# Attention's neighbour lists built earlier: sorted in the second product, eight of fifteen tiles' lists in the convolution

## The chip, the cores and the metric

The kernel runs on one core of one Trainium2 chip. A time is the device time of one execution in microseconds (us); three runs of the kernel before gave 1941.38, 1943.07 and 1949.31 us, and the median, 1943.07 us, is the figure to compare with. The profile is one further execution, recorded by the hardware profiler. It names the engines PE (matrix products; PEld its weight loads), DVE (vector), ACT (scalar), POOL (GpSimd) and SP (which here only issues DMAs). Each engine carries out its own instructions in the order in which the program gives them.

## The reference, cut to what matters

Four graph layers follow one another on x of shape 8 x 2048 x 64, with a random 0/1 adjacency of 2048 nodes whose entries are dense in its first rows and columns and sparse elsewhere. Each layer normalises x, applies ReLU, and adds its result to x.

- Layer 0: hyperedge attention, and a product of the adjacency with the features.
- Layer 1: a Chebyshev graph convolution. With A the adjacency, it forms A h and A (A h), and applies to h, A h and 2 A (A h) - h a weight that is a sum over 16 embedding values of each node.
- Layer 2: three steps, each a product of the adjacency with the state, then a small two-layer network.
- Layer 3: attention of each node over its neighbours:

```
adj = adj.at[jnp.diag_indices(N)].set(1.0)
e = leaky_relu(e_src[:, :, None] + e_dst[:, None, :]); e = adj[None] * e
h_prime = einsum('bij,bjd->bid', softmax(e, axis=-1), h)
```

Layer 3 needs, for every node, a list of its neighbours. The lists depend on the adjacency alone, so they can be built at any time before layer 3.

## The kernel before, in words

Nodes are held in 16 tiles of 128 (`NT`, `P`), a chunk is 512 nodes (`CW`), and the eight batches with 64 features make a row of 512 floats. The adjacency is not multiplied densely: nodes 0 to 383 are three dense "hub" tiles, and the rest are blocks that a list names (`LISTED`, 13 blocks for tile 0, then 7, 6, 5 and 4 or 3). Class `Feed` runs such a product. For each listed block it gathers 128 rows by an indirect DMA from POOL (line 2615), ACT rounds them to a high part (`part_hi`, 2632), DVE subtracts to get the low part (`part_lo`, 2633), and PE multiplies both into `acc`. DVE then adds the node's own row (`z`, 2676).

The stages that matter, with their place in the profiled execution:

- **Second product** (`layer1_near`, about 607 to 713 us): A h, tile by tile, through `Feed`. The convolution's first part for one column pair (`early`) follows it.
- **Convolution** (`convolution_near`, about 740 to 1225 us): over four chunks ("places") in the order 1, 0, 2, 3; in each, over four batch pairs q; in each, over eight blocks b taken by twos. Each (b, half) takes a PSUM bank `pk` (six buffers), two PE products, one DVE instruction for `y` (bias and embedding, line 1835; three buffers), and an addition of `y` into `half` (line 1842). The additions are on POOL, except those of the last block (`own = b == NBLK - 1`), which are on DVE. While one place is convolved, `product(place + 1)` advances the third product, A (A h), for the next chunk, by `advance()` twice per two blocks. Finished pairs are folded into x by PE (`fold_up`) some blocks later through the list `waiting`. The last place has no product ahead and sends layer 2's first messages instead.
- **Layer 2** (`layer2_near`, about 1225 to 1665 us): three steps of 16 tiles, each through `Feed`, with messages for the next step sent to DRAM after each tile (`u`, line 1874). The third step also projects and scores the chunks for layer 3.
- **Layer 3** (`layer3_near`, from about 1665 us).

The lists are made by a generator, `neighbours` (line 1994 on), all of it within the first two steps of layer 2. First it sorts the nodes by degree (`ranks`, line 483, then `by_rank`, line 527), and stores the order in DRAM (`order3`). Then, for tiles 1 to 15 of the sorted nodes, POOL gathers the 128 rows of links (2018), DVE multiplies them with the column numbers (2022), and takes the largest eight by MAX8 (2028), removing them with MATCH_REPLACE (2031) where more than eight are needed. `NEAR` gives the neighbours per tile, so tiles 1 to 8 need 3, 2, 2, 2, 2, 1, 1, 1 rounds of MAX8, and tiles 9 to 15 one each. `near_step()` calls the generator once per group of listed blocks, 22 times a step; what is left is drained ahead of the third step.

The order of the work is what the program's text gives, with a planner that moves an instruction where its buffers and operands are ready earlier or later in the planner's own reckoning; generators are how the text interleaves one stage with another.

Of the kernel before, what the change touches and what calls it, by code (L numbers as in the profile page):

```python
# [7 lines left out]
F = mybir.dt.float32  # L8
BF = mybir.dt.bfloat16

F12 = mybir.dt.float32r
I32 = mybir.dt.int32
# [7 lines left out]
P = 128  # L20
NB = 8
N = 2048
D = 64
NP = NB // 2
NT = N // P
R = P // NP
CW = 512
# [5 lines left out]
NBLK = DE * D // P  # L33

HELD = [16, 15, 10, 6, 3, 1, 1, 1, 1, 1, 1, 1]


NEAR = [None, 20, 14, 12, 10, 9, 8, 8, 7, 6, 6, 5, 5, 4, 4, 3]
TIED = [1 + sum(n > j for n in NEAR[1:]) for j in range(NEAR[1] + 1)]
FIRST = [sum(NEAR[1:t]) for t in range(NT + 1)]  # L40
# [6 lines left out]
F16 = mybir.dt.float16  # L47
# [88 lines left out]
class Kernel:  # L136
# [1527 lines left out]
    def layer1_near(self, slots, k2, far):  # L1664

        nc, tc, a = self.nc, self.tc, self.a
        self.steps = Steps(self, k2)
        lists = self.lists
        xe, xo = self.chebyshev(slots)
        ah = Halves(slots, "ah", ("q4", "q5"), True)  # L1670
        lo, hi = slice(0, D), slice(D, P)
        ident = self.ident
        lists.open(far.enter_context(
            tc.tile_pool(reuse_waits="tile", name="dense", bufs=1, side="right")
        ))
        with (
            tc.tile_pool(reuse_waits="tile", name="k1", bufs=1) as k,
            tc.tile_pool(reuse_waits="tile", name="conv_ps", bufs=1, space=PSUM) as ps,
        ):
            conv = Conv(self, slots, k, ps)  # L1680
            with tc.tile_pool(reuse_waits="tile", name="cheb", bufs=2) as w:
                hub = Hub(w, "first_hub")
                for t in range(HUBS):
                    hub.fill(self, t, ah(t))

                def turn(t):
                    s = slice(t * P, (t + 1) * P)
                    pz = ps.tile([P, NP, P], F, name="pz", tag="pk", bufs=6)
                    for q in range(NP):
                        nc.tensor.transpose(pz[:, q], ah(t)[:, q * P : (q + 1) * P], ident)  # L1690
                    for i in range(2):
                        qs = slice(2 * i, 2 * i + 2)
                        nc.scalar.copy(xo.tiles[i][lo, :, s], pz[lo, qs])
                        nc.vector.tensor_copy(xe.tiles[i][hi, :, s], pz[hi, qs])

                feed = Feed(self, lists, w, self.sent[0], lambda jt: ah(jt))
                for t in range(NT):
                    acc = ps.tile([P, CW], F, name="acc", bufs=2)
                    feed.target(acc, t, hub)
                    if t < HUBS:  # L1700
                        nc.scalar.copy(ah(t), acc)
                        lists.hub.fill(self, t, ah(t))
                    else:
                        feed.finish(ah(t), ah(t), acc, t)
                    nc.sync.dma_start(self.sent[1][t * P : (t + 1) * P], ah(t))
                    if t > 0:
                        turn(t - 1)
                    if t == NT // 2:
                        conv.begin()
                turn(NT - 1)  # L1710
                for _ in range(8):
                    next(conv.early)
            self.convolution_near(slots, k, ps, conv)

    def convolution_near(self, slots, k, ps, conv):
# [7 lines left out]
        with tc.tile_pool(reuse_waits="tile", name="conv", bufs=2) as w:  # L1723
# [60 lines left out]
            for _ in conv.early:  # L1784
                pass
            steps.prepare(bank)
            for place, ch in enumerate(chunks):
# [16 lines left out]
                for q in range(NP):  # L1804
# [6 lines left out]
                    for blk in range(0, NBLK, 2):  # L1811
# [15 lines left out]
                        for b in (blk, blk + 1):  # L1827
                            for half in range(2):
                                acc = accs[half]
                                new = begun or b > 0  # L1830
                                y = w.tile([P, CW], F, name="y", bufs=3) if new else acc
                                if begun:
                                    nc.vector.tensor_mul(y, pks[b, half], emb[:, b])
                                else:
                                    nc.vector.scalar_tensor_tensor(  # L1835
                                        y, pks[b, half], bias[:, b : b + 1], emb[:, b],
                                        op0=OP.add, op1=OP.mult,
                                    )
                                if new:
                                    own = b == NBLK - 1  # L1840
                                    add = nc.vector if own else nc.gpsimd
                                    add.tensor_add(acc, acc, y)  # L1842
# [39 lines left out]
    def layer2_near(self, slots, k2):  # L1882
# [3 lines left out]
        with (  # L1886
# [5 lines left out]
            own_w, seen, bias = self.steps.own, self.steps.seen, self.steps.bias  # L1892
            other = Hub(k, "other_hub")
            hubs = [lists.hub, other, lists.hub]
            near = self.neighbours(k, lambda: ps.tile([P, CW], F, name="p2"), slots)
            last = Scores(self, slots, k, w, ps)
            accs, late = {}, []

# [92 lines left out]
                    pass  # L1991
            last.end()

    def neighbours(self, k, bank, slots):

        nc = self.nc
        order = k.tile([P, 2, NT], I32, name="order")
        w = Parts(slots.tile([P, 2 * N], F, name="sort", tag="q4"))  # L2000
        rank = self.ranks(w, bank, 1, NEAR[1])
        yield
        self.by_rank(w, bank, rank, order)
        nc.sync.dma_start(self.order3, order)
        yield
        near = self.near
        words = slots.tile([P, 2, N], F, name="near_rows", tag="q4")
        rows = words[:, 0].bitcast(BF).rearrange("p (i n) -> p i n", i=2)
        named = words[:, 1].bitcast(F16).rearrange("p (i n) -> p i n", i=2)
        words = slots.tile([P, 2, N], F, name="line", tag="q5")  # L2010
        whole = words[:, 0].bitcast(I32)
        line = words[:, 1, : N // 2].bitcast(F16)
# [3 lines left out]
        for t in range(1, NT):  # L2016
            raw, row = rows[:, t % 2], named[:, t % 2]
            nc.gpsimd.indirect_dma_start(
                raw, None, self.links[:],
                bass.IndirectOffsetOnAxis(ap=order[:, 1, t : t + 1], axis=0),  # L2020
            )
            nc.vector.tensor_mul(row, raw, line)
            yield
            most = -(-NEAR[t] // 8)
            top = k.tile([P, 24], F, name="top", bufs=2)
            for i in range(most):
                eight = top[:, 8 * i : 8 * i + 8]
                nc.vector.max(out=eight, in_=row)
                yield
                if i + 1 < most:  # L2030
                    nc.vector.match_replace(
                        out=row, in_to_replace=eight, in_values=row, imm_value=0.0
                    )
# [647 lines left out]
class Conv:  # L2681
# [5 lines left out]
    def __init__(self, kern, slots, k, ps):  # L2687
# [19 lines left out]
        for j in range(2):  # L2707
# [9 lines left out]
        self.accs = [  # L2717
            [k.tile([P, CW], F, name=f"early{q}_{half}") for half in range(2)]
            for q in range(self.EARLY)
        ]  # L2720
        self.early = self.first_part()

    def bank(self):
# [18 lines left out]
    def first_part(self):  # L2742

        nc = self.nc
        s = slice(self.CHUNKS[0] * CW, (self.CHUNKS[0] + 1) * CW)
        for q in range(self.EARLY):
            for b in range(NBLK):
                for half, src in enumerate(self.xs):
                    pk = self.bank()
                    self.kern.mm(pk, self.w01[half][:, b * P : (b + 1) * P], src(q)[:, s])  # L2750
                    acc = self.accs[q][half]
                    y = self.k.tile([P, CW], F, name="early_y", bufs=2) if b else acc
# [502 lines left out]
```

## Time and profile before

| What | us |
|---|---|
| Median of three runs | 1943.07 |
| The profiled execution's own time | 1993.83 |
| Its span, first to last instruction | 1992.1 |
| PE busy over the span | 1714.6 (86%) |
| DVE busy | 1407.7 (71%) |
| POOL busy | 1047.7 (53%) |
| ACT busy | 819.8 (41%) |
| MAX8, 21 instructions | 48.0 |
| MATCH_REPLACE, 6 instructions | 13.7 |
| The lists' multiplications, 15 instructions | 18.3 |
| Last blocks' additions on DVE, 30 instructions | 33.4 |
| Additions of `y` on POOL, 180 instructions into `half` | 230.9 |

Shares of busy time are averages over stages with different limits, so the stages are read one by one: for a stretch of time, the view of windows gives the busy microseconds of every engine with the number of instructions, the PE clock granted, and the share of time that the DMA engines were busy. A group of instructions is shown as its line, engine and operation, what it writes and reads, its count, the busy microseconds and the mean in ns of one, and then the idle time of its engine just ahead of it with what ended that idle time. The view of waits lists who waited for whom. The chain of work that ended last is followed back from the last instruction; in this execution it reaches back to about 1260 us. The profiler slows the program: the profiled execution is 2.6% longer than the median.

### The profile page before, as it was taken

The page shows a single profiled execution, that of the slowest core. Times are in us where ns is not written, and L with a number is a line of the kernel's source. Part 1 is how long each engine was busy: PE and PEld are TensorE (multiplying, and loading weights), DVE is VectorE, ACT ScalarE, POOL GpSimd, SP SyncE. Part 2 cuts the span into 40 slices and gives each one's busy share as a digit, 9 for nine tenths or more (in the row PEclk, how much of TensorE's full clock was granted, in tenths as well). Part 3 has the DMA queues.
Part 4 walks back from the last instruction along what each step waited for, and adds up shares of the span by engine and source line. Part 5 has one row for each costly group of instructions (what it writes and reads, how often), then busy time and mean ns, then how long its engine had stood idle before and what let it go on. Part 6 is the DMA issues. An engine that isn't in the chain of part 4 may idle for free. (4 is left out here: it accounts for less than half of the span.)

```text
span 1992.1 us, 22431 instructions
## 1 busy us (share of the span) xinstructions
PE 1714.6 (86%) x7094; PEld 979.9 (49%) x7098; DVE 1407.7 (71%) x2307; ACT 819.8 (41%) x1650; POOL 1047.7 (53%) x1007
## 2 busy tenths in 40 slices
PE   6888999898888788999999998788787899398884
PEld 2446766663234544444444443466576665244432
DVE  6888788764667787677766566889776675276774
ACT  5722445445566643212120101555555663185300
POOL 1101466668645645776755554563663440767760
PEclk8888999998897997999999998899799898698997
DMA  9641223336436753242220211687677674746555
GB/s 342 262 117 45 75 93 113 103 110 217 127 134 188 238 178 106 64 122 69 74 85 27 88 50 54 218 255 240 201 246 246 190 236 147 249 122 187 169 152 189
DMA packets 127226, 305.22 MB, mean 153 GB/s; under 512 B 29536, under 2 KB 33392, under 8 KB 121968
## 3 DMA queue, kind: packets, MB, share of 16 engines
q0 software_dynamic: 45328, 149.60, 24.8%
q1 hardware_dynamic: 79456, 149.81, 22.2%
q10 hardware_dynamic: 2304, 4.20, 0.6%
q8 instruction: 60, 0.98, 0.2%
q14 instruction: 78, 0.64, 0.1%
HBM read 240.40 MB, written 63.14 MB: 152 GB/s over the span
## 5 line engine op out<-in xcount | busy, mean ns | idle before, releaser
L2615 POOL DMA_INDIRECT raw<-sent,index x300 | 321.3, 1071 | 302.0 <-DVE part_lo L2633 124.6
L2632 ACT CAST part_hi<-raw 128x512 fp32r<-128x512 f32 x352 | 213.0, 619 | 336.0 <-PE acc L177 226.9
L2633 DVE TENSOR_TENSOR part_lo<-raw,part_hi 128x512 fp32r<-128x512 f32 x352 | 264.3, 775 | 113.5 <-ACT part_hi L2632 60.7
L177 PE MATMUL pk<-q,w 128*128 128x512 f32 (+1 forms) x768 | 307.6, 619 | 2.0 <-DVE q L1731 0.9
L1842 POOL TENSOR_TENSOR half<-half,y 128x512 f32<-128x512 f32 x180 | 230.9, 1312 | 117.2 <-DVE y L1835 116.5
L177 PE MATMUL acc<-q,ident 128*128 128x512 f32 x416 | 209.4, 629 | 42.1 <-issue 17.3
L177 PE MATMUL acc<-part_lo,weights 128*128 128x512 f32 x365 | 169.0, 465 | 38.0 <-DVE part_lo L2633 32.2
L177 PE MATMUL acc<-part_hi,weights 128*128 128x512 f32 x365 | 174.4, 481 | 28.4 <-issue 14.1
L177 PEld LDWEIGHTS pk<-q,w 128*128 128x128 f32 (+1 forms) x768 | 117.5, 193 | 156.3 <-issue 121.5
L1835 DVE SCALAR_TENSOR_TENSOR y<-pk,bias,q 128x512 f32<-128x512 f32 x210 | 148.0, 743 | 55.5 <-PE pk L177 37.5
L2944 POOL DMA_INDIRECT ring<-f_rows,near x121 | 138.0, 1141 | 70.2 <-issue 29.9
L177 PEld LDWEIGHTS acc<-q,ident 128*128 128x128 f32 x416 | 78.9, 200 | 121.5 <-issue 70.9
L177 PEld LDWEIGHTS acc<-part_lo,weights 128*128 128x128 f32 x365 | 74.1, 203 | 91.7 <-DVE part_lo L2633 61.4
L2324 POOL TENSOR_TENSOR q<-q,beta 128x512 f32<-128x512 f32 x57 | 76.1, 1337 | 71.3 <-DVE beta L2300 32.9
L177 PEld LDWEIGHTS acc<-part_hi,weights 128*128 128x128 f32 x365 | 73.2, 200 | 79.9 <-issue 49.6
L3015 DVE TENSOR_TENSOR q<-ring,e 128x1024 f32<-128x1024 f32 x58 | 70.1, 1218 | 30.2 <-remote 13.3
L177 PE MATMUL pp<-adj,x_ind_hi 128*128 128x512 f32 x256 | 90.5, 470 | 0.5 <-DVE q L872 0.3
L2601 ACT CAST hub_weights<-dense 128x384 fp32r<-128x384 uint8 x80 | 40.5, 511 | 88.5 <-PE acc L177 84.6
L292 DVE RECIPROCAL std<-std 128x512 f32<-128x512 f32 (+1 forms) x17 | 53.7, 3161 | 30.9 <-ACT std L291 30.9
L2324 POOL TENSOR_TENSOR q<-q,coef 128x512 f32<-128x512 f32 x57 | 63.1, 1108 | 21.2 <-DVE q L2347 16.9
L2532 POOL DMA_INDIRECT listed_raw<-in_adjT_dram,cell x60 | 63.4, 1057 | 16.5 <-issue 16.2
L177 PE MATMUL pp<-adj,x_ind_lo 128*128 128x512 f32 x256 | 72.0, 400 | 0.0
(504 smaller groups left out, 3485.9 us busy)
## 6 DMA issues: line engine op xcount, KB each, us to landing
rows<-in_adj_dram SPq DMA_DIRECT2D x16, 1024.0 KB
adj_t<-in_adjT_dram SPq DMA_DIRECT2D x64, 256.0 KB
own<-sent SPq DMA_DIRECT2D x52, 256.0 KB
raw<-sent SPq DMA_DIRECT2D x52, 256.0 KB
sent<-u SPq DMA_DIRECT2D x48, 256.0 KB
q<-x SPq DMA_DIRECT2D x9, 1024.0 KB
links<-squares POOLq DMA_DIRECT2D x16, 512.0 KB
sent<-q SPq DMA_DIRECT2D x32, 256.0 KB
```

Of the source, the lines that this page charges most:

```text
L177: self.nc.tensor.matmul(out, lhsT, rhs, start=start, stop=stop)
L292: nc.vector.reciprocal(std, std)
L1835: nc.vector.scalar_tensor_tensor(y, pks[b, half], bias[:, b : b + 1], emb[:, b], op0=OP.add, op1=OP.mult,)
L1842: add.tensor_add(acc, acc, y)
L2324: self.nc.gpsimd.tensor_tensor(x, x, by.unsqueeze(2).to_broadcast([P, NB, D]), op=OP.mult)
L2532: self.kern.behind(nc.gpsimd.indirect_dma_start(raw[:, i], None, rows, bass.IndirectOffsetOnAxis(ap=self.cell[:, c + i : c + i + 1], axis= ...
L2601: self.nc.scalar.copy(to, self.lists.dense[:, :, i * P : (i + 1) * P])
L2615: self.nc.gpsimd.indirect_dma_start(raw, None, self.rows[:], bass.IndirectOffsetOnAxis(ap=self.lists.index[:, c : c + 1], axis=0),)
L2632: nc.scalar.copy(hi, raw)
L2633: nc.vector.tensor_sub(lo, raw, hi.bitcast(F))
L2944: self.nc.gpsimd.indirect_dma_start(to, None, self.kern.f_rows[:], bass.IndirectOffsetOnAxis(ap=index, axis=0))
L3015: nc.vector.tensor_tensor(y.rearrange("n i (b f) -> n i b f", b=NB), block[:, i : i + 2, : NB * D].rearrange("n i (b f) -> n i b f", b=NB) ...
```

## The change

The sort moves into a new function, `order_nodes`, which is advanced at tiles 2, 3 and 4 of the second product. `neighbours` now takes the order, a range of tiles and its buffers, gathers one tile ahead, and multiplies in place. Tiles 1 to 8 (`NEAR_EARLY = 9`) are listed in the convolution from its second place on, once per two blocks; tiles 9 to 15 in layer 2, which reads the order back from DRAM. The last blocks' additions, on DVE until now, join the others on POOL. The two buffers of the convolution's early part become one tile that the lists' rows use afterwards.

```diff
+NEAR_EARLY = 9
...
+                sorting = self.order_nodes(conv.bank, conv.order)
                 feed = Feed(self, lists, w, self.sent[0], lambda jt: ah(jt))
                 for t in range(NT):
...
                         turn(t - 1)
+                    if t > 1:
+                        next(sorting, None)
...
+                if place == 1:
+                    words = k.tile([P, 4 * CW], F, name="near_rows", tag="early", bufs=1)
+                    near = self.neighbours(
+                        steps.k, conv.order, range(1, NEAR_EARLY),
+                        words.bitcast(BF).rearrange("p (i n) -> p i n", i=2),
+                        words.bitcast(I32), w.tile([P, N], F16, name="line", bufs=1),
+                    )
...
                                 if new:
-                                    own = b == NBLK - 1
-                                    add = nc.vector if own else nc.gpsimd
-                                    add.tensor_add(acc, acc, y)
+                                    nc.gpsimd.tensor_add(acc, acc, y)
+                        next(near, None)
                         if q == NP - 1 and not ends:
...
+            for _ in near:
+                pass
             while waiting:
...
-            near = self.neighbours(k, lambda: ps.tile([P, CW], F, name="p2"), slots)
+            order = k.tile([P, 2, NT], I32, name="order")
+            nc.sync.dma_start(order, self.order3)
+            words = slots.tile([P, 2, N], F, name="near_rows", tag="q4")
+            near = self.neighbours(
+                k, order, range(NEAR_EARLY, NT),
+                words[:, 0].bitcast(BF).rearrange("p (i n) -> p i n", i=2),
+                words[:, 0].bitcast(I32), words[:, 1, : N // 2].bitcast(F16),
+            )
...
+    def order_nodes(self, bank, order):
+        rank = order[:, 1].bitcast(F)
+        with self.tc.tile_pool(reuse_waits="tile", name="sort", bufs=1) as w:
+            self.nc.vector.tensor_copy(rank, self.ranks(w, bank, 1, NEAR[1]))
         yield
+        with self.tc.tile_pool(reuse_waits="tile", name="sorted", bufs=1) as w:
+            self.by_rank(w, bank, rank, order)
         yield
+        self.nc.sync.dma_start(self.order3, order)
+        yield
+
+    def neighbours(self, k, order, tiles, rows, whole, line):
+        nc, near = self.nc, self.near
         nc.gpsimd.iota(whole, pattern=[[1, N]], base=1, channel_multiplier=0)
         nc.vector.tensor_copy(line, whole)
         yield
+        def fetch(i):
+            if i < len(tiles):
+                t = tiles[i]
+                nc.gpsimd.indirect_dma_start(
+                    rows[:, i % 2], None, self.links[:],
+                    bass.IndirectOffsetOnAxis(ap=order[:, 1, t : t + 1], axis=0),
+                )
+
+        fetch(0)
+        for i, t in enumerate(tiles):
+            fetch(i + 1)
+            row = rows[:, i % 2].bitcast(F16)
+            nc.vector.tensor_mul(row, rows[:, i % 2], line)
             yield
...
+        early = k.tile([P, 4, CW], F, name="early", tag="early", bufs=1)
+        self.accs, self.ys, self.turn = [[early[:, 0], early[:, 1]]], early[:, 2:], 0
+        self.order = k.tile([P, 2, NT], I32, name="order")
```

More of the change, by code (lines that the diff above doesn't have):

```diff
@@ L1786, in convolution_near @@
             steps.prepare(bank)
+            near = iter(())
             for place, ch in enumerate(chunks):
@@ L1992, in layer2_near @@
             last.end()
[L1994 to L2001, printed above, removed]
+    def order_nodes(self, bank, order):
+        rank = order[:, 1].bitcast(F)
+        with self.tc.tile_pool(reuse_waits="tile", name="sort", bufs=1) as w:
+            self.nc.vector.tensor_copy(rank, self.ranks(w, bank, 1, NEAR[1]))
         yield
-        self.by_rank(w, bank, rank, order)
-        nc.sync.dma_start(self.order3, order)
+        with self.tc.tile_pool(reuse_waits="tile", name="sorted", bufs=1) as w:
+            self.by_rank(w, bank, rank, order)
         yield
[L2006 to L2012, printed above, removed]
+        self.nc.sync.dma_start(self.order3, order)
+        yield
+    def neighbours(self, k, order, tiles, rows, whole, line):
+        nc, near = self.nc, self.near
         nc.gpsimd.iota(whole, pattern=[[1, N]], base=1, channel_multiplier=0)
@@ L2015, in neighbours @@
         yield
[L2016 to L2022, printed above, removed]
+        def fetch(i):
[10 more added lines that the diff above has]
+            nc.vector.tensor_mul(row, rows[:, i % 2], line)
             yield
@@ L2025, in neighbours @@
             top = k.tile([P, 24], F, name="top", bufs=2)
-            for i in range(most):
-                eight = top[:, 8 * i : 8 * i + 8]
+            for j in range(most):
+                eight = top[:, 8 * j : 8 * j + 8]
                 nc.vector.max(out=eight, in_=row)
                 yield
-                if i + 1 < most:
+                if j + 1 < most:
                     nc.vector.match_replace(
@@ L2716, in __init__ @@
         self.xs = kern.chebyshev(slots)
[L2717 to L2720, printed above, removed]
+        early = k.tile([P, 4, CW], F, name="early", tag="early", bufs=1)
+        self.accs, self.ys, self.turn = [[early[:, 0], early[:, 1]]], early[:, 2:], 0
+        self.order = k.tile([P, 2, NT], I32, name="order")
         self.early = self.first_part()
@@ L2751, in first_part @@
                     acc = self.accs[q][half]
-                    y = self.k.tile([P, CW], F, name="early_y", bufs=2) if b else acc
+                    y = self.ys[:, self.turn % 2] if b else acc
+                    self.turn += b > 0
                     nc.vector.scalar_tensor_tensor(
```

## The prediction

> **What bounds the kernel now.** I first cut the span into stages by the lines at work, and read the view of windows: the second product, the convolution's second and third places, and layer 2's steps 0, 1 and 2.
>
> ```profile
> core 0: us, PE busy (x) PEld busy (x) DVE busy (x) ACT busy (x) POOL busy (x), PEclk, DMA share, GB/s
> 607.00:713.00 106.00, 87.21 (x328) 55.62 (x326) 78.10 (x128) 72.62 (x155) 65.56 (x60) 0.91 0.76 231
> ...
> 891.00:1003.00 112.00, 111.07 (x353) 46.95 (x353) 78.18 (x97) 18.80 (x37) 72.52 (x60) 1.00 0.26 79
> 1003.00:1112.00 109.00, 107.97 (x346) 44.02 (x344) 76.00 (x99) 13.68 (x28) 66.08 (x53) 1.00 0.19 57
> ...
> 1245.00:1385.00 140.00, 114.58 (x615) 89.61 (x616) 119.85 (x169) 80.81 (x160) 74.54 (x67) 0.93 0.74 236
> 1385.00:1525.00 140.00, 113.50 (x580) 89.31 (x579) 110.38 (x147) 80.45 (x160) 76.44 (x71) 0.90 0.74 238
> 1525.00:1665.00 140.00, 126.35 (x592) 87.51 (x591) 88.24 (x161) 78.53 (x160) 57.69 (x58) 0.94 0.63 201
> ```
>
> The convolution is PE's: 99% busy, DVE about 70%. In steps 0 and 1 nobody is full: DVE 120 and 110 of 140, PE 114. Step 2 does more PE work (126) in the same 140 with DVE at 88. So steps 0 and 1 are long for their PE work, and I asked what PE waits for there, by the waits of 1252 to 1390, then of 1385 to 1525 (total us, times, longest).
>
> ```profile
> PE acc L177 <- DVE part_lo L2633: 9.6, 10, 2.8
> PE pz L1920 <- DVE z L2676: 4.8, 5, 2.2
> ```
>
> ```profile
> PE acc L177 <- DVE part_lo L2633: 13.5, 8, 2.7
> PE pz L1920 <- DVE z L2676: 1.5, 2, 0.8
> ```
>
> With 1.7 that step 0's groups put to MAX8 itself, PE idles 16.1 us for DVE in step 0 and 15.0 in step 1; step 2's group of the same products shows 0.2. The longest waits, 2.7 and 2.8 us, are about one list instruction long. These are DVE's groups in 1245 to 1385 and in 1385 to 1525:
>
> ```profile
> L2028 DVE MAX8 top<-q 128x8 f32<-128x2048 f16 x10 | 22.8, 2285 | 0.0
> L2031 DVE MATCH_REPLACE8 q<-top,q 128x2048 f16<-128x2048 f16 x6 | 13.7, 2276 | 0.0
> ...
> L2022 DVE TENSOR_TENSOR q<-q,q 128x2048 f16<-128x2048 bf16 x5 | 6.1, 1219 | 0.9 <-issue 0.9
> ```
>
> ```profile
> L2028 DVE MAX8 top<-q 128x8 f32<-128x2048 f16 x11 | 25.2, 2287 | 0.0
> L2022 DVE TENSOR_TENSOR q<-q,q 128x2048 f16<-128x2048 bf16 x10 | 12.2, 1216 | 0.0
> ```
>
> Last, DVE's groups in the convolution, 800 to 1225:
>
> ```profile
> L1835 DVE SCALAR_TENSOR_TENSOR y<-pk,bias,q 128x512 f32<-128x512 f32 x206 | 145.3, 743 | 55.5 <-PE pk L177 37.5 <-POOL half L1842 16.1 <-PE side L177 0.5
> L2633 DVE TENSOR_TENSOR part_lo<-raw,part_hi 128x512 fp32r<-128x512 f32 x42 | 51.3, 1228 | 30.1 <-ACT part_hi L2632 30.1
> L1842 DVE TENSOR_TENSOR half<-half,y 128x512 f32<-128x512 f32 x30 | 33.4, 1119 | 7.8 <-POOL half L1842 5.9
> ```
>
> DVE's idle time before `y` is mostly for PE: slack to put lists into. A `part_lo` takes 1.23 us here and 0.69 in layer 2.
>
> **What the Trainium skill says.** "SBUF — State Buffer", Who interferes with whom: a DVE instruction with two SBUF inputs contends with a GpSimd one that reads SBUF, and one with at most one SBUF input outside the two-port modes does not. The trace agrees: `part_lo` and DVE's additions (1.12 us) are stretched beside POOL's additions, and `y` from PSUM (0.743) is not. MAX8 and MATCH_REPLACE read one tensor, so I leave them at 2.28 us in the convolution; no run yet shows that. The lists' multiplication reads two and may pay as `part_lo` does. "TensorE: Matmul & The Clock Gate", Architectural detail: DVE is a strict FIFO, so a list instruction holds all behind it; the waits of 2.7 us fit. "Perfetto Trace Analysis", Identifying the Most-Contended Engine: PE's matmul busy share overstates nearness to its peak. PEld is at 42% in the convolution and 64% in layer 2, so the 99% means "no waiting", not "no slack".
>
> **The change part by part**, on the profiled 1993.83 us.
>
> *Layer 2.* The lists of tiles 1 to 8 leave: 8 x 1.22 + 14 x 2.29 + 6 x 2.28 = 55.5 us of DVE. So does the sort: nine additions of 0.52 make 4.7, the wide comparison 2.3, the small rest about 7.9; 14.9 in all, of which 12.5 fell between 1246 and 1271 and the rest in the convolution. Tiles 9 to 15 stay, 7 x (1.22 + 2.29) = 24.6. They need 15 calls and step 0 has 22, so step 1 becomes free of lists.
>
> What is that worth? First way: PE's idle time for DVE. Step 1's 15.0 goes; in step 0 list and sort work falls from 56 us (12.5 + 43.5) to about 27, so half of 16.1 goes, 8. Together 23. Second way: pace. From tile 3 to tile 15 `z` comes every 6.2 us in both steps (1303.9 to 1378.7, 1436.3 to 1510.9). PE was about 88% busy there; at 97% that is 5.6 us, so 12 x 0.6 = 7 in step 1 and, with lists in a third of the tiles, 4 in step 0. The starts: from the last message to tile 3's `z` step 2 took 37 us, step 1 51.5 and step 0 58. About 4 of the differences are messages that step 2 lacks; the rest, 10 and 17, is list and sort work. Step 1 gets 10 back, step 0 a share of 14.7 in 26.4, 9.5. Together 30. I take 27; bounds 15 (what the chain of work puts on list lines, 7% of step 0 and up to 4% of step 1) and 55 (69 us of DVE work at DVE's 80% of the time).
>
> *Second product.* The sort's 14.9 us enter tiles 2 to 4, about 643 to 663. DVE is 12 of 20 busy there, waiting for the first gathers, so 8 hide it and 7 remain; as tiles also wait for DMA I charge 5 (bounds 0 and 15). The six `pk` banks are shared with the transposes, and two or three small products go in between: nothing, if the planner places them once their operands are there. The store of the order is one more DMA on SP, ahead of a tile's store and the next own row; its 0.5 us of issue hides behind gathers. If it waited for the sort, own rows would be late by that.
>
> *Convolution.* In its second place calls 1 to 15 put three lists in: 1.16 for the line of numbers, 3 x 1.22 + 7 x 2.29 + 4 x 2.28, together 30 us. In the third: 5 x 1.22 + 7 x 2.29 + 2 x 2.28 = 27. DVE's additions leave each (7.8, 8.9). So DVE goes from 78 to 100 of 112, and from 76 to 94 of 109: 90% and 86%. A call comes once per two blocks, about 7 us of PE; it stands behind that pair's four `y`, where DVE waits up to 4.2 us for the next bank, and ahead of the next `part_lo`, for which PE waits in order. Most of 2.3 us hides. I charge 5 us (28 instructions, 0.2 each); bounds -3 (DVE no longer waits for POOL behind its own additions, 5.9) and 40 (all 57 less 16.7).
>
> POOL receives 32 additions (30 into `half`, two of the early part) of 1.31, 2.6 us per q of 28. It goes from 72.5 to 86 of 112 with three gathers, in the first place from 76 to 86 of 106. `fold_up` comes one to two pairs of blocks later, which hides them; without that cover a pair costs 2.6. In the last q nothing hides it: two additions of 1.3 in place of 0.7, some 0.6. The eight gathers (1.05) cost nothing on a POOL with a quarter free. Each now waits for the MAX8 that last read its half of the buffer, since the multiplication is in place; queued behind it on POOL are additions, and behind those DVE's `y`. With calls 7 us apart that MAX8 is done. Layer 2's reload of the order is one small DMA on SP and repeats a line of numbers, 1.16 us of DVE: in the 27.
>
> Sum: -27 + 5 + 5 + 0.6 = -16.4, so 1977.4. The median is 0.9745 of the profiled time: -16, 1927.
>
> **The rivals.** *Layer 2 follows DVE* (16 in 100): late low parts hold the ring of gathers (POOL waited 23.7 us for `part_lo` in step 1) and all compounds: -55 + 6 = -49, or -48 of the median, 1895. For: both were half idle without a cause of their own. Against: lists are only 4 to 7% of the chain.
>
> *Nothing to collect* (18): PE, DMA (74% busy at 238 GB/s) and message latency set the pace, -15 + 14 = -1, 1942. For: the chain gives 9.4% of step 1 to the stores of messages and 41% to PE's `acc`. Against: step 2's short start.
>
> *The convolution turns DVE's* (11), slower: at 90% in order, each list instruction lands just ahead of a `y` or `part_lo` that PE needs, and PE waits for nearly all of it. 40 + 5 + 0.6 - 27 = +18.6, about 1961. It decides from 21 us in the convolution, 0.8 per list instruction. For: layer 2 shows such waits, and PE has no spare time here. Against: six banks, and gaps of up to 4.2 us.
>
> That the lists are not moved (all drained at one place) is under 1 in 100: 30 calls fit the 48 hooks.
>
> **How the numbers follow.** The forecast has 55, own range 1914 to 1937. Half a per cent, 9.7 us, is about what a measurement tells from no change: below 1933.4 lie 46 of the 55, all of the first rival and 3 of the second: 0.65. Within it 9, 14 and 1: 0.24. Slower, 1 of the second rival and 10 of the third: 0.11. Leaving out most of the two ends gives 1899 to 1950.
>
> **What would show it.** Step 1 at 120 us or less with no MAX8 in it and PE's waits for `part_lo` under 4; `z` every 5.6 us or less in it; step 0 some 12 shorter; the second product 5 longer with the sort in it; places two and three of the convolution within 5 us of 112 and 109, PE still at 98% or more, MAX8 at 2.29 us, the multiplication at up to 1.8; 210 additions on POOL into `half`. I am wrong if PE in these places idles for `part_lo` or `y` by more than 10 us, or if step 1 without lists stays near 135.

## The result: slower by 1.3%

The changed kernel took 1970.65 us (median of four runs, 1967.78 to 1972.61) beside 1944.19 for the kernel before: a ratio of 1.0131, interval 1.0110 to 1.0153. The forecast was 1927, range 1899 to 1950.

For the comparison of stages I use a second profile of the kernel before, taken with the first experiments (span 1947.2 us; the execution took 1948.97). The runs of this study fell on chips of different speed: on one the kernel before takes 1943.57 us, on three others 1992.12, 1986.65 and 1997.70, and its first profile (1993.83) looks like one of the latter: its last stages, "the rest" below, took 475.5 us, those of the later profiles on the three chips 466 to 475. So ratios are given within one chip, and totals and layer 2 are compared between profiles of like chips. In us:

| Stage, first and last mark | Before | Changed | Difference |
|---|---|---|---|
| start to the second product's first hub product | 606.9 | 610.6 | +3.7 |
| second product, to the first `early` | 106.5 | 111.2 | +4.7 |
| early part, to the first `half` | 72.8 | 74.0 | +1.2 |
| convolution, to the last fold | 440.1 | 479.3 | +39.2 |
| to layer 2's first message product (`pn`) | 50.4 | 53.1 | +2.7 |
| messages of layer 2, first to last `pn` | 226.0 | 198.0 | -28.0 |
| the rest | 444.5 | 444.7 | +0.2 |

The sum is +23.7. Layer 2 gave what was forecast, the sort cost what was forecast, and the convolution took 39 us instead of 5. Where in the convolution? The view of windows of the changed kernel, four stretches in its first place and the first quarter of its second, whose first `half` begins at 913.3 (busy us of each engine in the order of the header):

```profile
core 0: us, PE busy (x) PEld busy (x) DVE busy (x) ACT busy (x) POOL busy (x), PEclk, DMA share, GB/s
...
850.00:875.00 25.00, 21.50 (x63) 9.29 (x64) 25.00 (x27) 5.28 (x11) 22.04 (x19) 0.93 0.31 88
875.00:900.00 25.00, 18.69 (x53) 7.75 (x52) 25.00 (x24) 4.30 (x9) 15.32 (x15) 0.88 0.52 123
900.00:925.00 25.00, 21.40 (x62) 8.29 (x60) 24.86 (x23) 1.72 (x3) 14.75 (x12) 0.91 0.33 106
925.00:950.00 25.00, 21.61 (x52) 8.12 (x53) 24.00 (x24) 6.52 (x12) 13.66 (x11) 0.80 0.42 140
```

The same view of the kernel before, over about the same work (its second place begins at 877.3):

```profile
840.00:865.00 25.00, 25.00 (x85) 11.37 (x84) 18.86 (x23) 6.73 (x14) 18.69 (x17) 1.00 0.38 104
865.00:890.00 25.00, 24.96 (x80) 10.72 (x80) 17.76 (x23) 3.33 (x7) 17.74 (x15) 1.00 0.43 124
890.00:915.00 25.00, 25.00 (x80) 10.44 (x78) 19.41 (x22) 6.86 (x13) 12.82 (x11) 1.00 0.29 98
```

DVE went from 71 to 78% busy to 96 to 100%, PE from full to 75 to 86%, and PE's granted clock from 1.00 to 0.80 to 0.93. DVE's groups of the changed kernel between 825 and 950 say what fills it (name, count, busy us, mean ns):

```profile
L2051 DVE MAX8 top<-near_rows 128x8 f32<-128x2048 f16 x14 | 31.9, 2282 | 0.0
...
L2655 DVE TENSOR_TENSOR part_lo<-raw,part_hi 128x512 fp32r<-128x512 f32 x20 | 26.0, 1306 | 0.0
...
L2058 DVE COPY near<-top 128x8 f32<-128x8 f32 (+6 forms) x8 | 7.6, 950 | 0.0
```

All fourteen MAX8 of the convolution stand here (823.2 to 935.1): ten in the *first* place and four in the first quarter of the second. The text gives them out from the second place on, two places long; the planner had their operands and a free buffer and moved them ahead, into the place in which the product ahead is the longest (13 + 7 + 6 + 5 listed blocks). From mark to mark, the first `half` of a place or quarter, the first place lost 26.4 us (117.5 for 91.1) and the first quarter of the second 10.3 (41.7 for 31.4). From there to the last place, where the prediction had put most of the lists, it takes 197.7 us (955.0 to 1152.7), as before (197.6, 908.7 to 1106.3). The last place lost 2.4.

What PE waited for in the whole convolution, changed kernel (total us, times, longest):

```profile
PE pk L178 <- DVE y L1847: 11.9, 7, 3.9
PE acc L178 <- DVE part_lo L2655: 11.1, 4, 4.9
PE side L178 <- POOL half L1852: 4.3, 1, 4.3
```

And before:

```profile
PE acc L177 <- DVE part_lo L2633: 2.2, 1, 2.2
PE side L177 <- DVE half L1842: 2.1, 1, 2.1
```

One such wait in the timeline of the changed kernel (start, us, engine, what; in brackets the idle time before it):

```profile
879.78 2.29 DVE L2051 MAX8 top<-near_rows 128x8 f32<-128x2048 f16 x1
882.00 0.67 DVE L2655 TENSOR_TENSOR part_lo<-raw,part_hi 128x512 fp32r<-128x512 f32 x1
...
882.72 0.49 PE L178 MATMUL acc<-part_lo,weights 128*128 128x512 f32 x1 [2.52 <-DVE part_lo L2655]
```

PE stood 2.52 us, about the length of the MAX8 (2.29) that DVE did ahead of the `part_lo`. The 39.2 us split in two: over the convolution PE was idle 31.6 us (479.0 less 447.39) where it was 6.4 before (440.0 less 433.64), +25; and its products took 447.39 us for 433.64, +14, with a mean granted clock of 0.95 for 0.99. "TensorE: Matmul & The Clock Gate", Part 1 of the Trainium skill, says that PE is throttled by default and that activity releases it; the trace agrees as far as the clock fell in the stretches where PE idled. Here each us of waiting went with about half a us of slower products.

The clock also fell once without idle time, some 20 us into the last place, in some executions and not in others. The kernel before, first and second profile:

```profile
1131.00:1141.00 10.00, 9.90 (x39) 5.00 (x40) 5.41 (x9) 0.59 (x1) 5.77 (x5) 1.00 0.08 29
```

```profile
1126.00:1136.00 10.00, 9.90 (x24) 4.68 (x23) 5.28 (x8) 0.59 (x1) 6.03 (x5) 0.66 0.05 17
```

Between the two the waits are the same (6.4 us), but the convolution takes 435.6 and 440.1 us. By an estimate (a stretch times what its clock lacks to 1.00) this dip cost 0 us in the first profile and in the kernel without lists below, 3.4 in the second profile, 5.1 in the changed kernel, and 1.7 to 5.1 in the others. Less the dip, the two profiles of one kernel agree within 1.1 us (three such pairs), so differences of the convolution below some 4 us say little unless the dips are taken off. What sets it off no run shows.

In layer 2 the gain is where it was looked for. PE's waits in step 1, before (1374 to 1497) and changed (1415 to 1520):

```profile
PE acc L177 <- DVE part_lo L2633: 7.2, 7, 2.0
PE pz L1920 <- DVE z L2676: 4.9, 4, 1.6
```

```profile
PE pz L1940 <- DVE z L2698: 1.2, 1, 1.2
...
PE acc L178 <- DVE part_lo L2655: 0.8, 4, 0.2
```

From the last `z` of step 0 to that of step 1 it takes 105.6 us for 123.3, and from tile 3 to tile 15 `z` comes every 5.35 us for 5.98. Here, too, the planner moved lists ahead: all seven remaining MAX8 run from 1287.2 to 1326.0, before the first message product at 1328.2.

### The profile page after: what moved, and what is told of

It is laid out like the page before. It is cut to its first block, busy times and chain, and to the rows that moved or that the text cites. A ratio compares the mean times of both kernels' runs of the same rounds, so it can differ in the third digit from the quotient of the medians.

```text
span 1970.9 us, 22503 instructions
## 1 busy us (share of the span) xinstructions
PE 1717.0 (87%) x7098; PEld 975.1 (49%) x7098; DVE 1385.1 (70%) x2277; ACT 819.0 (42%) x1650; POOL 1078.1 (55%) x1040
## 5 line engine op out<-in xcount | busy, mean ns | idle before, releaser
L2637 POOL DMA_INDIRECT raw<-sent,index x300 | 310.5, 1035 | 262.6 <-DVE part_lo L2655 151.7
L178 PE MATMUL pk<-q,w 128*128 128x512 f32 (+1 forms) x768 | 317.7, 636 | 10.3 <-DVE y L1847 8.8
L1852 POOL TENSOR_TENSOR half<-half,y 128x512 f32<-128x512 f32 x210 | 269.6, 1313 | 103.9 <-DVE y L1847 103.3
L178 PE MATMUL acc<-q,ident 128*128 128x512 f32 x416 | 202.6, 613 | 24.3 <-DVE q L3056 17.8
L178 PEld LDWEIGHTS pk<-q,w 128*128 128x128 f32 (+1 forms) x768 | 119.6, 198 | 170.5 <-issue 117.5
```

The source lines that it names most:

```text
L178: self.nc.tensor.matmul(out, lhsT, rhs, start=start, stop=stop)
L1852: nc.gpsimd.tensor_add(acc, acc, y)
L2637: self.nc.gpsimd.indirect_dma_start(raw, None, self.rows[:], bass.IndirectOffsetOnAxis(ap=self.lists.index[:, c : c + 1], axis=0),)
```

## The experiments

Theory 1: DVE, crowded in the convolution's first place, is the loss. Theory 2: the 30 additions that went to POOL are. Theory 3: a list instruction costs PE the same wherever it stands, in e3's text its full length, from e4 on about half a microsecond. The names e0 to e11 in the expectations are those in brackets here.

**The kernel before, again** (e0). It gave the second profile, used above.

> The kernel before, profiled once more. The first profile of it (1993.83 us) lay 2.6% above its own timed runs, the one of the changed kernel (1972.61) on them. If that first execution was merely a slow one, this one comes near 1944, layer 3 takes about 244 us from its first gather to its last stage as in the changed kernel (262 in the first profile), and the convolution, from the first half to the last fold, again 436 us. If the profiler itself slows the kernel before, it is near 1994 again.

1948.97 us in its one run, span 1947.2. So the first profile was of a slower execution, and the opening's statement that the profiler slows the program by 2.6% doesn't hold. The last stages took 444.5 us, as in the changed kernel (444.7). The convolution took 440.1 us where 436 was expected; the dip of the clock is most of the difference.

**The additions back on DVE** (e1, from the changed kernel):

```diff
-                                    nc.gpsimd.tensor_add(acc, acc, y)
+                                    own = b == NBLK - 1
+                                    add = nc.vector if own else nc.gpsimd
+                                    add.tensor_add(acc, acc, y)
```

> The changed kernel with the last blocks' additions put back on DVE; sort and lists stay where the change has them. Theory 1 (DVE is full for 125 us because the planner moved the eight lists forward into the convolution's first place): 30 more instructions on DVE don't help, the convolution stays at 475 us or more, total 1965 to 1980, slower than before. Theory 2 (the additions on POOL hold up DVE's y and PE's folds): the convolution returns towards 445 us and the total to 1925 to 1945.

1968.72 us, ratio 1.0111 (1.0073 to 1.0149); convolution 484.1 us. The loss stays with the additions gone from POOL, so Theory 2 falls.

**No list in the convolution** (e2). All fifteen in layer 2; sort early and additions on POOL as in the change:

```diff
-NEAR_EARLY = 9
+NEAR_EARLY = 1
...
-                if place == 1:
+                if place == 1 and NEAR_EARLY > 1:
```

> The changed kernel with all fifteen lists in layer 2 again; the sort stays in the second product and all additions on POOL. Theory 1: the convolution is back at 433 to 440 us, layer 2 is long again, and the total is within 10 us of before, 1935 to 1950. Theory 2: the convolution stays at 460 us or more and the total above 1960.

1951.69 us, ratio 1.0041 (1.0023 to 1.0060). The convolution takes 438.9 us, about as before (440.1 and 435.6), so the lists are nearly its whole loss. Not all of it: PE idles 10.0 us here for 6.4 before, and its two long waits are longer than before (2.1 and 2.2), with no list instruction beside them:

```profile
PE side L178 <- POOL half L1852: 4.3, 1, 4.3
PE acc L178 <- DVE part_lo L2655: 3.3, 1, 3.3
```

Against the first profile of before, which had no dip of the clock either, that is 3.3 us for the rest of the change. Layer 2's messages take 210.5 us: the sort's move, with the new way of fetching rows ahead, gives 15.5 of the 28.0.

**The lists held where the text puts them** (e3). Every instruction of the convolution's lists is kept in program order:

```diff
-            nc.vector.tensor_mul(row, rows[:, i % 2], line)
+            pin(nc.vector.tensor_mul(row, rows[:, i % 2], line))
...
-                nc.vector.max(out=eight, in_=row)
+                pin(nc.vector.max(out=eight, in_=row))
```

and likewise for the iota (it writes the column numbers), the copies, the gathers and MATCH_REPLACE; `pin` is `self.behind`, which tells the planner to keep the order.

> The changed kernel with each instruction of the lists in the convolution held behind what the program text has ahead of it on its engine, so that the planner can't move it forward: the lists then stand in the second and third places, one list instruction per two blocks. Theory 1: DVE is below 95% in every 25 us of the convolution, which takes 435 to 445 us, and the total is 1922 to 1938, faster than before. Theory 3 (PE has no spare time anywhere in the convolution, so that lists cost their full length wherever they stand): the convolution stays at 470 us or more and the total at 1960 or more.

1945.00 us, ratio 0.9999 (0.9975 to 1.0023). MAX8 now runs from 912.6 to 1106.5 and the convolution takes 455.6 us: 23.7 of the 39.2 are gone with nothing changed in the program but the order in which the lists stand. Theory 1 holds for that part; DVE is at most 95% busy in any 25 us. But 15.5 stay, three times the prediction's 5, and the total isn't below before. PE's waits in this convolution:

```profile
PE pk L178 <- DVE y L1847: 4.7, 3, 3.5
PE side L178 <- POOL half L1852: 4.3, 1, 4.3
PE acc L178 <- DVE part_lo L2655: 3.3, 1, 3.3
```

With 3.3 for `q` and 1.6 for `q` of the fold these are 17.2 us for 5.9 before. Of these the 4.3 and the 3.3 aren't the lists': they stand in e2 as well, and the wait for `part_lo` ends at 827 us, ahead of DVE's first list instruction (894.8). DVE's group of multiplications shows one cause of the others, a queue held by a DMA:

```profile
L2045 DVE TENSOR_TENSOR near_rows<-near_rows,line 128x2048 f16<-128x2048 bf16 x8 | 9.7, 1213 | 7.0 <-DMA near_rows<-links,order 7.0
```

DVE stood 7.0 us for the first rows (and 3.7 for the iota just before), with `y` queued behind; that is where the wait of 3.5 us for `y` is:

```profile
907.51 1.23 DVE L2045 TENSOR_TENSOR near_rows<-near_rows,line 128x2048 f16<-128x2048 bf16 x1 [6.98 <-DMA near_rows<-links,order]
908.65 1.40 DVE L1847 SCALAR_TENSOR_TENSOR y<-pk,bias,q 128x512 f32<-128x512 f32 x2
909.45 3.78 PE L178 MATMUL pk<-q,center 128*128 128x512 f32 x4 [3.49 <-DVE y L1847]
```

**The third and fourth places** (e4). The last place has no product ahead, so no `part_lo`:

```diff
-                if place == 1:
+                if place == 2:
```

> As e3, the list instructions held in program order, but between the blocks of the convolution's third and fourth places instead of its second and third. Theory 1 (the lists cost what they take from DVE where the product ahead's eviction, part_lo, needs it too; the last place has no product ahead): the convolution falls from e3's 455.6 us to about 445, the total to 1930 to 1938, ratio to before about 0.995. Theory 3 (each list instruction costs the convolution about 0.55 us wherever it stands, because TensorE then waits for y): the convolution stays at 452 to 458, the total at 1942 to 1948.

2000.75 us, ratio 1.0050 (1.0020 to 1.0079), on a slower chip. The convolution takes 450.0 us, and 452.7 when the same kernel ran again (below). Theory 1 asked for about 445, Theory 3 for 452 to 458: the place matters little once the lists are spread (less the dip, 448 and 449 us for e3's 450), and PE's waits are the same list as above (`y` 4.6, `half` 4.3, `part_lo` 3.4, `q` 2.8).

**Behind the product ahead** (e5). As the pinned kernel, with the list instruction given out after the second `advance()`:

```diff
-                        next(near, None)
                         if q == NP - 1 and not ends:
                             load_emb(place + 1, blk)
                         advance()
+                        next(near, None)
```

> As e3, but each list instruction is given out behind the product ahead's eviction of its block instead of ahead of it. If it is this order on DVE (2.3 us of MAX8 ahead of part_lo) that holds TensorE, the convolution falls to about 447 us and no wait for part_lo is left above 1 us; the total is about 1937. If it is the sum of DVE's work, the convolution stays at 453 to 458 us and the total at 1943 to 1948.

2016.03 us, ratio 1.0113 (1.0081 to 1.0145); convolution 462.0, worse than either answer expected. The longest wait for `part_lo` stays (3.4 us), as it must if it is e2's, and the waits for `y` grow from 4.7 to 8.2, perhaps because the MAX8 now stands nearer to the next pair's `y`. Ahead of `part_lo` was the better of the two.

**The small copies on ScalarE**, and the last block's last additions on DVE (e6, from the third-place kernel):

```diff
-            pin(nc.vector.tensor_copy(near[:, FIRST[t] : FIRST[t + 1]], top[:, : NEAR[t]]))
+            nc.scalar.copy(near[:, FIRST[t] : FIRST[t + 1]], top[:, : NEAR[t]])
```

> As e4, with two edits: the eight small copies of a list run on ScalarE, and the very last block of the convolution adds its last product on DVE again. If the copies' stretched times (1.48 us mean in e3, beside GpSimd's additions) lie on DVE's path, the convolution falls by 3 to 8 us below e4's and the last wait of TensorE for GpSimd's half (4.3 us) goes to about 2; total 1925 to 1935, faster than both kernels. If they are hidden, it is within 2 us of e4.

2007.44 us, ratio 1.0080 (1.0048 to 1.0111); convolution 454.1, 4.1 more than e4's and 1.4 more than e9's, the same kernel run again, where 3 to 8 less was expected. The copies leave DVE (6.9 us there, 1.6 on ScalarE), and 5.3 us come back: the eight multiplications take 15.0 for 9.7. It seems that the wait moved to the next instruction that has to share with POOL. The wait for the last `half` became 3.7, now for DVE.

**Rows ready before their place** (e7). As the third-place kernel, with the iota, its copy and the first two gathers given out one place earlier and left free:

```diff
-        pin(nc.gpsimd.iota(whole, pattern=[[1, N]], base=1, channel_multiplier=0))
-        pin(nc.vector.tensor_copy(line, whole))
+        nc.gpsimd.iota(whole, pattern=[[1, N]], base=1, channel_multiplier=0)
+        nc.vector.tensor_copy(line, whole)
...
+        fetch(0, lambda made: made)
+        fetch(1, lambda made: made)
         yield
```

> As e4, with what the first multiplication of the lists waits for (the iota, its copy, the gathers of the first two tiles' rows) given out one place earlier and left free; MAX8 and the rest stay held in program order in places three and four. In e3 the DVE stood 3.7 us for the iota and 7.0 us for those rows with y queued behind it, and TensorE lost 3.5 us for y there and then ran at a lower granted clock. If this stall is a third of the 15 us that pinned lists still cost, the convolution falls 4 to 7 us below that of e9 and the wait for y to about 1 us; the total is 0.2 to 0.4% below e9's. If each list instruction costs by itself, the convolution stays within 2 us of e9's.

1987.51 us, ratio 0.9986 (0.9965 to 1.0006). The convolution takes 446.0 us, 6.7 below the same kernel without this edit (452.7, on the same chip), and DVE no longer stands for rows. PE's waits:

```profile
PE side L178 <- POOL half L1853: 4.3, 1, 4.3
PE acc L178 <- DVE part_lo L2659: 4.2, 1, 4.2
...
PE pk L178 <- DVE y L1848: 1.2, 2, 0.9
```

The wait for `y` fell from 4.7 to 1.2, as expected, and the medians of the timed runs, 1987.51 and 1994.82, agree with 6.7. Of it 1.7 us is the dip of the clock; against e4, with the same dip, the gain is 4.0. So Theory 3 is wrong for 4 to 5 us: that part was a stall on a DMA, not a price of list instructions. What is left above e2 is 7.1 us, 5.4 less the dip, for 28 list instructions: 0.19 us each by this estimate.

**No list beside the fold** (e8). As that, without list instructions in the first pair of blocks of a q in the third place:

```diff
-                        if place >= 2:
+                        if place >= 2 and (ends or blk > 0):
                             next(near, None)
```

> As e7, and in the third place no list instruction in the first pair of blocks of a q, where the fold of the q before runs on DVE (q L1735 and q L1744, for which TensorE waited 3.3 and 1.6 us in e3). If these waits are the second part of the cost, the convolution falls another 3 to 5 us, to within 5 us of the kernel before, and the total is 0.5% below that of the kernel before on a chip where layer 2's messages take some 196 us, and about equal to it where they take 229.

1988.51 us, ratio 1.0007 (0.9987 to 1.0026); convolution 451.6, 5.6 more instead of 3 to 5 less. The timed runs show no such loss (1988.51 and 1987.51 us), and 3.4 of the 5.6 are the dip of the clock (5.1 us for e7's 1.7). The wait for `q` went from 3.4 to 2.8 only, and the last one, for POOL's `half`, from 4.3 to 6.3; more list work stands in the last place, which may be why.

**The third-place kernel and the changed kernel again** (e9 and e10), on the chip of these runs:

> The same kernel as e4, again, beside the two above. Theory A (e4's messages of layer 2 took 229.7 us against e3's 196.4 because the chip of that run moved data more slowly, 221 against 258 GB/s): on a chip where the kernel before takes about 1943 us, layer 2's messages take 195 to 202 us and the total is 1938 to 1946; on one where it takes about 1992, 229 us and 2000. Theory B (lists in the later places themselves delay layer 2): 225 to 232 us whatever the chip.

> The changed kernel itself, beside the three above on the same chip. The convolution takes 479 us again, since DVE's crowding in its first place doesn't depend on the chip. If the chip is one where the kernel before takes about 1943 us, the messages take about 198 us and the ratio is 1.010 to 1.014. If it is one where the kernel before takes about 1992 us, the messages gain only some 11 us on it (229 us) and the ratio is 1.017 to 1.022.

1994.82 us, ratio 1.0032 (1.0001 to 1.0064), and 2020.27 us, 1.0135 (1.0048 to 1.0222). The changed kernel's convolution takes 478.3 us (479.3 on the other chip), with waits of 13.5 for `y` and 12.2 for `part_lo`: the crowding doesn't depend on the chip. Layer 2 does: its messages take 222.8 and 220.2 us here, so not the lists' place but the chip makes the difference to 196.4 and 198.0. The windows of the messages on the faster chip (lists pinned) and on this one (third place):

```profile
1304.00:1501.00 197.00, 184.54 (x1081) 151.44 (x1079) 128.70 (x198) 138.04 (x276) 116.02 (x113) 1.00 0.82 258
```

```profile
1306.00:1529.00 223.00, 193.12 (x1076) 156.63 (x1075) 128.19 (x198) 138.71 (x277) 113.23 (x113) 0.95 0.71 228
```

The DMA engines moved 228 GB/s for 258, and PE waited 11.0 us for `part_hi`, which needs the gathered rows, where it waited 4.5. This suggests that with DVE freed the rows are next in line. Against the first profile of before (240.7 us) the changed kernel gains 20.5 us here, against 28.0 on the faster chip. I had expected 229 us for both, and a ratio of 1.017 to 1.022 for the changed kernel.

**Rows ready, and the last additions on DVE** as in the kernel before (e11):

```diff
-                                    nc.gpsimd.tensor_add(acc, acc, y)
+                                    own = b == NBLK - 1
+                                    add = nc.vector if own else nc.gpsimd
+                                    add.tensor_add(acc, acc, y)
```

> As e7 (446.0 us in the convolution), with the last block's additions of every q on DVE again, as in the kernel before. If their move to GpSimd is what leaves the 4.3 us that TensorE waits for the last half (2.1 before) and the 4.2 for part_lo (2.2 before), the convolution falls to about 442 and the total to 0.3 to 0.5% below the kernel before; if DVE now has too little room (33 us more of work on it), it stays at 446 or rises to 450, and the ratio is 0.998 to 1.002.

1996.10 us, ratio 0.9994 (0.9970 to 1.0019); convolution 447.3 us. The wait of 4.2 for `part_lo` stays, that for the last `half` only falls to 3.6, now for DVE, and DVE is busy 351.5 us for 326.7: nothing is won. So the move of the additions explains 0.7 of the 2.2 us by which the last wait had grown. Ahead of the last additions POOL does the 2048 numbers of layer 2's list line, which the change makes a second time and the kernel before doesn't have here:

```profile
1233.08 1.83 POOL L2033 IOTA q<- 128x2048 int32 x1
1234.89 8.36 POOL L1855 TENSOR_TENSOR half<-half,y 128x512 f32<-128x512 f32 x6
1242.06 1.74 DVE L1855 TENSOR_TENSOR half<-half,y 128x512 f32<-128x512 f32 x1 [0.47 <-POOL half L1855]
1243.85 1.97 PE L178 MATMUL side<-half,fold 128*64 128x512 f32 x2 [3.59 <-DVE half L1855]
```

Its 1.83 us are of the size of the 1.5 that stay; e1, e2, e3 and the changed kernel have the same iota there. No run takes it away, so this is argued and not shown. No version beat the kernel before by more than can be measured.

## Why the prediction was wrong, by its own steps

- **What bounds the kernel**: right. Steps 0 and 1 were long because PE waited for DVE there, and the waits left with the lists and the sort.
- **Layer 2, -27**: right, -28.0, with some luck in step 0. In step 1 the terms fit: pace 7 (measured 12 x 0.63 = 7.6), start 10 (51.6 to 41.4 us from step 0's last `z` to tile 3's). In step 0 I had lists in a third of the tiles; they were done before the first message product, so its pace gained 7.0 for 4, and its start, which held them, 5.5 for 9.5 (57.4 to 51.9 us from the last message to tile 3's `z`). The two misses nearly cancel. That more than half (15.5) came with the sort's move and the rows fetched ahead was not in my sum, which gave the lists four fifths of the DVE work that left.
- **Second product, +5**: right, +4.7.
- **The convolution, +5**: this step failed, and its first failure is the place. "In its second place calls 1 to 15 put three lists in" took the text for the order of the work. The planner moved them into the first place and the first quarter of the second, where DVE then had no free microsecond in 850 to 900, and PE waited in order behind it. Held in the places assumed, the lists left 23.7 of the 39.2 us behind. The evidence was in the prediction itself: of the sort, which the text of the kernel before puts into layer 2, 2.4 us had run in the convolution. Had I asked from when on buffer and operands are free, the first place would have been the answer.
- **The price of a list instruction, 0.2 us**: too small where the lists stand as I had assumed, 15.5 us over 28 instructions, or 0.55. But the price itself came near (0.19, estimated after e7); what the sum lacked were other terms. 4 to 5 us was the stall of DVE's queue on the first gather (I had counted gathers on POOL, and not whom their arrival holds on DVE), and about 3 us stand without any list (e2). The copies `near<-top` I left out altogether: eight took 7.6 us of DVE in the changed kernel and 11.8 when pinned, beside 0.16 each at their fastest.
- **The tail, +0.6**: mis-sized. PE waited 4.3 us for POOL's last `half` where it had waited 2.1 for DVE's: +2.2. With the additions back on DVE 3.6 stayed, so most of it isn't the additions'; I had charged layer 2's second line of numbers to DVE (1.16 us), and not its 1.83 us of POOL just here.
- **MAX8 at 2.28 us beside POOL**: right (2282 ns), and with it what "SBUF — State Buffer", Who interferes with whom, of the Trainium skill says: a DVE instruction with at most one SBUF input, outside the two-port modes, doesn't contend with GpSimd. The multiplication reached 1.81 us, as forecast.
- **POOL's additions hidden**: right to within some 3 us. The kernel without lists in the convolution, with all 210 additions on POOL, idles PE 3.6 us longer than before, 2.2 of it in the tail.
- **The scaling by 0.9745**: wrong, as e0 showed. That moved the sum by 0.4 us.
- **The rivals**: "The convolution turns DVE's" had the mechanism, the waits of PE for `y` and `part_lo`, and the size, 40 for 39.2, but named the wrong place and had too small a chance. Its 1961 lacked the +3.7 ahead of the second product, which has no known cause, +1.2 in the early part and +2.7 ahead of the first message. That its 40 came out is luck: it was all 57 us of list work less 16.7, in two places where in the end only four of the fourteen MAX8 stood.

Why the repaired kernels only break even: pinned, the change pays 6.6 us in the second product, 15.5 in the convolution, 5.3 in the two small stages and gets 29.6 back in layer 2 (196.4 for 226.0), -2.2 in these five; the timed runs show no difference.

## What to carry to other kernels

Where a planner orders the work, an edit's place in the text needn't be where its instructions land (here a whole place earlier); look up from when on their buffers and operands are free, and cost them there. A move from a stage that waits for an engine into one where another engine is 99% busy pays only as far as the first engine has gaps that nothing in order depends on: here 55 us of DVE work bought about 14 us in layer 2 (210.5 to 196.4) and cost about 17 in the convolution even when spread (438.9 to 455.6), 7 with the rows ready (446.0). Before an instruction goes into a full in-order queue, have its DMA land a stage earlier. And before waits are put down to a change, look which of them stand without it.

## What the runs showed of the hardware

- A lost microsecond of PE cost about 1.5: over the convolution 25 us more of idle time came with 14 us of slower products, at a granted clock of 0.80 to 0.93 in 850 to 950. The clock records of the traces hold two grants, full and half, the half ones in pieces of 3.4 us and their multiples. In the convolution they make 12.6 us in the second profile of before and 43.2 in the changed kernel. One such piece also came where PE was 99% busy (clock 0.66 in 1126 to 1136).
- A copy of 128 x 8 numbers took 0.16 us in layer 2 and up to 3.0 us in the convolution, beside POOL's additions of about 1.3 us. "SBUF — State Buffer", Who interferes with whom, of the Trainium skill says that copies can enter a mode that needs the ports shared with GpSimd and that the one issued later blocks in full. The trace fits, and with the copies taken away the next instruction with two inputs, the multiplication, was longer in their place (mean 1.21 to 1.87 us, longest 4.08).
- Chips differ by 2 to 3% on this kernel (1943.57 to 1997.70 us for the same program). The changed kernel on two of them differed in layer 2's messages (198.0 and 220.2 us) and in the last stages (444.7 and 466.9), where the DMA engines are 60 to 82% busy, and not in the convolution (479.3 and 478.3), where they are 23 to 24% busy.
